# Two graph layers on one core: layer 0's small sums moved from GpSimd to VectorE, and transposes of single pairs one step later

## The chip, the cores and the metric

The kernel runs on one core of a Trainium2 chip. The metric is device time in microseconds (us), lower is better. Engines: PE is TensorE, PEld its weight loads, DVE is VectorE, ACT is ScalarE, POOL is GpSimd, SP is SyncE. "L307" is line 307 of the kernel in question.

## The reference, cut to what matters

```python
# x: 4096 x 512, adj: 4096 x 4096
def layer0(x, adj, weight):
    bw = sign(weight); ba = max(sign(x), 0)
    return relu(adj @ (ba @ bw.T))
x = layernorm(x + layer0(x, adj, w0))

def layer1(x, adj, weight, bias, node_w, edge_w):
    node_att = softmax(x @ node_w, axis=0)
    h = x @ edge_w
    e = where(adj > 0, h @ h.T, NEG_BIG)
    return adj * (node_att * softmax(e, axis=1)) @ (x @ weight) + bias
x = layernorm(x + layer1(...))
```

The whole program has these stretches: layer 0's aggregation `adj @ xw`, then `h`, then the products `h @ h.T` with their softmax statistics, then layer 1's aggregation. The change touches the first and the third.

## The kernel before

Layer 0's aggregation goes by blocks of 128 rows. A block's adjacency arrives in two halves, each half in two chunks. For each chunk, ScalarE makes `hi` (the rounded value), VectorE makes `lo` (the rest), and PE multiplies both. Beside that runs work for layer 1, two pieces per block: `premask` turns pieces of the adjacency into bf16 masks and stores them.

```python
def premask(queue, left):
    if loaded and (len(bufs) == 2 or len(pieces) == left):
        (r, j, c), a = loaded.popleft()
        m = ...                                   # bf16 view of the same buffer
        tc.keep_in_program_order(nc.vector.tensor_scalar(m, a_, 0.0, NEG_BIG, ALU.is_le, ALU.mult))
        nc.gpsimd.dma_start(mask_d[r][:, c : c + 2, j, :], m)      # store, GpSimd's queue
        bufs.append(a)
    if len(pieces) > left:
        r, j, c = pieces.popleft()
        a = bufs.popleft()                        # must wait until the store from `a` has landed
        queue.dma_start(a, adj[...])              # in layer 0: ScalarE's queue
        loaded.append(((r, j, c), a))

def aggregate(b):
    ...
        for q in range(2):
            nc.scalar.copy(hi, aq)
            nc.vector.tensor_sub(lo, aq, hi.bitcast(F32))
            if q == 0:
                premask(nc.scalar, 28)
            for c in range(QC):                   # 8 x 2 matmuls
                nc.tensor.matmul(acc, hi[:, c, :], xw[:, kb, :], ...)
                nc.tensor.matmul(acc, lo[:, c, :], xw[:, kb, :], ...)
    nc.vector.scalar_tensor_tensor(xb, acc, 0.0, xb, ALU.max, ALU.add)
    layernorm([xb])
    nc.vector.tensor_tensor_reduce(scr, xb, nw_b, ..., accum_out=node_s[:, b : b + 1])   # node score
    nc.gpsimd.tensor_add(scr, xb, bias_b)                                               # bias add
    nc.gpsimd.dma_start(x1_d[ts(b, P), :], scr)
    return xb

def left(b, low, high):                           # once for each pair of blocks
    nc.gpsimd.tensor_sub(s3, l11, l21)
    nc.gpsimd.tensor_add(s1, l22, l21)
    nc.gpsimd.tensor_sub(s2, s1, l11)
    nc.gpsimd.tensor_sub(s4, l12, s2)
    nc.gpsimd.dma_start(to[:, 0, :], l11)         # four stores of operands
    ...
```

There are four buffers for the pieces, `pair` (two), `single` and `ends`. The build reorders instructions within an engine unless they are held with `keep_in_program_order`. In the products, a row's copy to SBUF is followed some "steps" later (calls of `between`) by its transposes on PE:

```python
class Single:
    def main(self, between):
        for i in range(BG):
            for k in range(KD):
                nc.tensor.matmul(pe[...], ...)
                if k % 2 and not (self.diag and i > 1):
                    between()                                     # one step
            nc.scalar.copy(src[:, lo * P :], pe[:, lo * P :])
            turns.append((now[0] + 2, lambda ...: self.mirror.turn(s, src, i)))   # transposes
            ...
```

## Time and profile before

| | before |
|---|---|
| time, median of the first 3 runs | 2068.59 us (2063.06 to 2071.97) |
| profiled execution, span | 2059.6 us |
| layer 0's aggregation, first to last matmul after the start-up | 58.9 to 577 us |
| products, first matmul to layer 1's first aggregation matmul | 684.0 to 1163.1 us |
| DVE / ACT / POOL busy | 67% / 33% / 25% |

The lines of the profile that matter are in the prediction, with how to read each. In a line of waits, "A <- B: total, times, longest" means that A's engine stood idle before A until B was done. In a timeline the columns are start, duration, engine, line, operation, output<-inputs, shapes, count, and in brackets the idle time before it and what ended that.

### The profile page before, as it was taken

How to read it: one execution, taken by the hardware profiler on the slowest of the kernel's cores; microseconds unless marked ns; L12 is line 12 of the kernel's file. 1: busy time of each engine (PE TensorE's matmuls, PEld its weight loads, DVE VectorE, ACT ScalarE, POOL GpSimd, SP SyncE). 2: the span in 40 equal slices, each digit the busy share in tenths (PEclk: the TensorE clock that was granted, in tenths of full speed). 3: DMA queues.
4: the chain of work that ended last, by engine and by line, in shares of the span. 5: the costliest groups of instructions: out<-in, count | busy, mean ns of one | idle time of the engine just before them, and what ended most of it. 6: DMA issues, size and time to landing. Idle time of an engine off the chain costs nothing.

```text
span 2059.6 us, 18124 instructions
## 1 busy us (share of the span) xinstructions
PE 1989.2 (97%) x6108; PEld 1104.0 (54%) x6108; DVE 1370.2 (67%) x1896; ACT 673.0 (33%) x1107; POOL 522.6 (25%) x603
## 2 busy tenths in 40 slices
PE   9999899999998999999999899999999999999997
PEld 6777777777853445555545444444444444444443
DVE  7655566665666457576747688688669666967734
ACT  5322232222310357666768431122111311221100
POOL 0443434343543011111112211241215111330101
PEclk9999999999999999999999999999999999999999
DMA  8877777777647558577859887676667766775421
GB/s 302 295 262 251 269 270 275 263 253 253 231 163 261 204 193 287 215 256 281 292 192 366 310 298 261 218 255 240 239 229 246 255 234 213 258 250 209 174 82 61
DMA packets 133644, 497.70 MB, mean 242 GB/s; under 512 B 14000, under 2 KB 14000, under 8 KB 125872
## 3 DMA queue, kind: packets, MB, share of 16 engines
q0 software_dynamic: 71488, 262.17, 34.2%
q1 hardware_dynamic: 54000, 206.07, 29.8%
q10 hardware_dynamic: 8064, 28.32, 4.0%
q8 instruction: 48, 0.79, 0.2%
q14 instruction: 44, 0.36, 0.1%
HBM read 376.96 MB, written 119.54 MB: 241 GB/s over the span
## 4 chain that ended last, share of the span: by engine, by line
PE 70%; DMA 9%; issue 7%; POOL 6%; DVE 4%; ACT 2%; ACTq 0%; POOLq 0%; SPq 0%; DVEq 0%
PE ps L850 37%; PE seven L664 11%; PE po L903 5%; DMA mask_d<-ends 4%; PE seven L98 4%; PE acc L300 3%; PE acc L299 3%; PE pe L595 2%; POOL scr L307 2%; PE pt L565 2%; DMA s_d<-slot 1%; DMA mask_d<-pair 1%; ACT hi L292 1%; DVE lo L294 1%; PE acc L236 1%
## 5 line engine op out<-in xcount | busy, mean ns | idle before, releaser
L850 PE MATMUL ps<-lent,lop 128*128 128x512 f32 x992 | 432.6, 592 | 0.0
L299 PE MATMUL acc<-xw,hi 128*128 128x512 f32 x960 | 390.9, 407 | 26.2 <-ACT hi L292 26.2
L300 PE MATMUL acc<-xw,lo 128*128 128x512 f32 x960 | 389.7, 406 | 11.1 <-DVE lo L294 10.9
L850 PE MATMUL ps<-slot,lop 128*128 128x512 f32 x800 | 351.9, 594 | 0.0
L850 PEld LDWEIGHTS ps<-lent,lop 128*128 128x128 f32 x992 | 188.3, 190 | 236.3 <-issue 231.8
L850 PEld LDWEIGHTS ps<-slot,lop 128*128 128x128 f32 x800 | 152.2, 191 | 190.0 <-issue 185.2
L294 DVE TENSOR_TENSOR lo<-at,hi 128x1024 fp32r<-128x1024 f32 x120 | 155.5, 1297 | 148.1 <-ACT hi L292 148.0
L292 ACT CAST hi<-at 128x1024 fp32r<-128x1024 f32 x120 | 125.9, 1049 | 320.4 <-PE acc L299 202.8
L299 PEld LDWEIGHTS acc<-xw,hi 128*128 128x128 f32 x960 | 188.4, 196 | 69.8 <-ACT hi L292 31.3
L300 PEld LDWEIGHTS acc<-xw,lo 128*128 128x128 f32 x960 | 188.4, 196 | 57.6 <-DVE lo L294 18.2
L854 DVE TENSOR_TENSOR over<-over,ps 128x512 f32<-128x512 f32 x168 | 113.5, 680 | 90.2 <-PE ps L850 90.2
L595 PE MATMUL pe<-hT 128*128 128x512 f32 (+3 forms) x384 | 132.3, 486 | 0.0
L767 ACT ACTIVATE lent<-lent 128x2048 f32<-128x2048 f32 x33 | 62.9, 1910 | 192.5 <-DVE lent L764 189.1
L536 ACT ACTIVATE line<-line,nmax_c 128x512 f32<-128x512 f32 x160 | 114.8, 724 | 33.1 <-DVE nmax_c L527 33.1
L767 ACT ACTIVATE slot<-slot 128x2048 f32<-128x2048 f32 x31 | 59.3, 1911 | 201.1 <-DVE slot L764 201.1
L903 PE MATMUL po<-over 128*128 128x512 f32 x256 | 115.9, 600 | 3.2 <-DVE xb L912 3.2
L527 DVE CUSTOM_DVE_ANT_0 line<-lent,slot 128x512 f32<-128x512 bf16 x144 | 93.0, 688 | 37.0 <-ACT slot L605 19.7
L764 DVE CUSTOM_DVE_ANT_1 slot<-slot,line 128x2048 f32<-128x2048 f32 x31 | 75.2, 2425 | 49.1 <-DMA slot<-s_d 47.6
L764 DVE CUSTOM_DVE_ANT_1 lent<-lent,line 128x2048 f32<-128x2048 f32 x33 | 83.0, 2519 | 23.4 <-DMA lent<-s_d 22.2
L664 PE MATMUL seven<-hT 128*128 128x512 f32 x192 | 89.5, 593 | 0.0
L565 PEld LDWEIGHTS pt<-ident,lent 128*128 128x128 f32 x422 | 52.0, 141 | 63.3 <-issue 39.6
L595 PEld LDWEIGHTS pe<-hT 128*128 128x128 f32 x384 | 64.6, 191 | 37.9 <-issue 31.0
(197 smaller groups left out, 2611.0 us busy)
## 6 DMA issues: line engine op xcount, KB each, us to landing
at<-in_adj_t_dram SPq DMA_DIRECT2D x60, 1024.0 KB, 6.3
lop<-lop_d SPq DMA_DIRECT2D x112, 512.0 KB, 3.6
lent<-in_adj_t_dram POOLq DMA_DIRECT2D x35, 1024.0 KB, 6.9
s_d<-slot POOLq DMA_DIRECT2D x34, 1024.0 KB, 7.6
lent<-s_d POOLq DMA_DIRECT2D x33, 1024.0 KB, 7.3
slot<-s_d POOLq DMA_DIRECT2D x31, 1024.0 KB, 7.8
slot<-in_adj_t_dram POOLq DMA_DIRECT2D x29, 1024.0 KB, 7.5
lent<-in_adj_dram SPq DMA_DIRECT2D x48, 512.0 KB, 5.6
```

The costliest lines, as they stand in the source:

```text
L292: nc.scalar.copy(hi, aq)
L294: nc.vector.tensor_sub(lo, aq, hi.bitcast(F32))
L299: nc.tensor.matmul(acc, hi[:, c, :], xw[:, kb, :], start=(kb == 0), stop=False)
L300: nc.tensor.matmul(acc, lo[:, c, :], xw[:, kb, :], start=False, stop=(kb == NB - 1))
L536: nc.scalar.activation(line, line, AF.Exp, bias=nmax_c[:, b, c : c + 1], scale=-1.0, accum_out=sum_c[:, b, c : c + 1])
L595: nc.tensor.matmul(pe[:, lo * P :], hT[:, k, ts(A * BG + i, P)], hT[:, k, (B * BG + lo) * P : (B + 1) * W], start=(k == 0), stop=(k == KD ...
L664: nc.tensor.matmul(ps, left[m][:, k, q, :], right[m][:, k, :], start=(first and k == 0), stop=(k == KD // 2 - 1), skip_group_check=not first,)
L764: nc.vector._custom_dve(TENSOR_ADD_SAT, out=q, in0=q, in1=mrow.unsqueeze(1).to_broadcast([P, BG, W]), s0=0.0, s1=-HUGE)
L767: nc.scalar.activation(q, q, AF.Exp)
L850: nc.tensor.matmul(ps, lop[:, c, ts(h, P)], rop[:, c, :], start=(c == 0), stop=(c == BG - 1))
L854: nc.vector.tensor_add(total[:, m, h, :], total[:, m, h, :], ps)
L903: nc.tensor.matmul(po, (lower if k // 2 else upper)[:, k % 2, ts(i, P)], w1_s[:, k, :], start=(k == 0), stop=(k == KD - 1),)
```

## The change

Its intent: GpSimd should only begin stores in layer 0, so that none stands behind arithmetic; and in the products, PE should come to a transpose later, when the copy it reads is done, with one step also at the end of each of the last two rows of a diagonal product (the other rows had it).

```diff
@@ aggregate
-            nc.gpsimd.tensor_add(scr, xb, bias_b)
+            nc.vector.tensor_add(scr, xb, bias_b)
@@ left
-            nc.gpsimd.tensor_sub(s3, l11, l21)
-            nc.gpsimd.tensor_add(s1, l22, l21)
-            nc.gpsimd.tensor_sub(s2, s1, l11)
-            nc.gpsimd.tensor_sub(s4, l12, s2)
+            nc.vector.tensor_sub(s3, l11, l21)
+            nc.vector.tensor_add(s1, l22, l21)
+            nc.vector.tensor_sub(s2, s1, l11)
+            nc.vector.tensor_sub(s4, l12, s2)
@@ Single.main
-                    if k % 2 and not (self.diag and i > 1):
+                    if k == KD - 1 or k % 2 and not (self.diag and i > 1):
                         between()
-                turns.append((now[0] + 2, lambda i=i, s=s, src=src: self.mirror.turn(s, src, i)))
+                turns.append((now[0] + 3, lambda i=i, s=s, src=src: self.mirror.turn(s, src, i)))
```

## The prediction

> **What bounds the kernel now.** I read the page's busy times and slices first, then busy time by stretch, then the waits of layer 0's aggregation, then each engine's timeline through one pair of its row blocks.
>
> ```profile
> PE 1989.2 (97%) x6108; PEld 1104.0 (54%) x6108; DVE 1370.2 (67%) x1896; ACT 673.0 (33%) x1107; POOL 522.6 (25%) x603
> PE   9999899999998999999999899999999999999997
> POOL 0443434343543011111112211241215111330101
> ```
>
> TensorE (PE) is busy 97% of 2059.6 us, so only its idle time and its slow-clock time can be won. The slices with an 8 or a lone dip lie mostly in the first quarter, exactly where GpSimd (POOL) is busiest. By stretch (columns: length, then busy us and count of each engine, granted clock, DMA share, GB/s):
>
> ```profile
> 140.00:240.00 100.00, 92.20 (x391) 73.75 (x390) 60.07 (x75) 28.42 (x35) 38.77 (x46) 0.95 0.76 264
> 340.00:440.00 100.00, 89.20 (x363) 71.06 (x362) 59.82 (x73) 25.82 (x32) 42.30 (x47) 0.91 0.75 259
> 517.00:577.00 60.00, 60.00 (x272) 49.37 (x271) 36.97 (x46) 18.54 (x23) 32.53 (x30) 1.00 0.62 224
> ```
>
> The last stretch is the same aggregation after the mask work has ended: no idle PE, clock 1.00. Before it PE idles 8 to 11% and also loses clock. From 59 to 577 us PE issues 1920 aggregation matmuls and 120-odd transposes. The matmuls start 0.227 us apart when nothing stalls (timeline, 240.14 then 240.37), so 1920 x 0.227 = 436 us, and transposes take some 19 us (0.6 for four). 518 - 455 leaves about 63 us lost. Cross-check: PE busy in those 518 us sums to 481, so 37 us idle; the clock averages 0.95, some 25 us more. Sum 62. From 577 us on, PE is nearly gapless, so a gain there is small, and what layer 0 wins simply moves the end forward.
>
> ```profile
> ACT hi L292 <- DMA mask_d<-ends: 74.5, 9, 9.9
> PE acc L299 <- ACT hi L292: 26.2, 12, 4.1
> ACT hi L292 <- DMA mask_d<-pair: 20.0, 5, 4.9
> PE acc L300 <- DVE lo L294: 10.9, 14, 2.2
> ```
>
> The 37 us are two lines: PE waits for ScalarE's (ACT) cast `hi` and then for VectorE's (DVE) `lo`; and `hi` waits for the landing of a mask store. ScalarE also issues the adjacency loads, in order, and a load into `ends` may not start until the mask stored from `ends` has landed; the cast behind it stands still. Why that store is late is in GpSimd's timeline:
>
> ```profile
> 275.40 0.73 POOL L317 TENSOR_TENSOR sums_l<-xb 128x256 f32<-128x256 f32 x1 [3.48 <-DVE xb L154]
> 276.09 0.72 POOL L321 DMA_DIRECT2D lop_d<-xb  x1
> 276.83 2.15 POOL L307 TENSOR_TENSOR scr<-xb,bias_b 128x512 f32<-128x512 f32 x1
> 278.94 1.19 POOL L318 TENSOR_TENSOR sums_l<-sums_l,xb 128x256 f32<-128x256 f32 x1
> 280.07 0.57 POOL L308 DMA_DIRECT2D x_d<-scr  x1
> 280.67 1.25 POOL L319 TENSOR_TENSOR sums_l<-xb,sums_l 128x256 f32<-128x256 f32 x1
> 281.87 0.77 POOL L323 DMA_DIRECT2D lop_d<-sums_l  x1
> 282.63 0.57 POOL L322 DMA_DIRECT2D lop_d<-sums_l  x1
> 283.19 0.71 POOL L272 DMA_DIRECT2D mask_d<-ends  x1
> ```
>
> The normalised row is there at 275.3; the mask of `ends` was ready at 279.5 and its store begins at 283.19, behind 5.3 us of arithmetic. It lands at 290.4, and ScalarE follows:
>
> ```profile
> 290.86 1.04 ACT L292 CAST hi<-at 128x1024 fp32r<-128x1024 f32 x1 [7.24 <-PE acc L300]
> ```
>
> Its buffer had been free since about 286.2 (the cast before started at 282.58, one chunk is 16 x 0.227 = 3.6 us). This recurs once in each pair of row blocks, some 12 times, at 4 to 7 us each.
>
> **What the Trainium skill says.** "GPSIMD Engine Reference", section 3.1, gives GpSimd about 2.6 cycles an element for a two-input add against VectorE's 1, a measured ratio of 1.96. Here the 128x512 add takes 2.18 us (median of 31) on GpSimd; a VectorE add of that shape takes 0.69 (layer 1's groups). The trace is worse than the page. "SBUF — State Buffer", section "Who interferes with whom", has VectorE and GpSimd exclude each other on a shared port pair, for two-port modes and for two-input VectorE operations against GpSimd reads. It agrees:
>
> ```profile
> L271 DVE TENSOR_SCALAR single<-single x13: 685/687/691, 93.0 to 515.2; 128x1024 bf16<-128x1024 f32 x13
> L271 DVE TENSOR_SCALAR ends<-ends x13: 1769/1778/1787, 101.2 to 523.1; 128x1024 bf16<-128x1024 f32 x13
> ```
>
> (Minimum/median/maximum ns.) The same mask operation takes 1.78 us every time it meets the bias add L307, and 0.69 where GpSimd only issues. "TensorE: Matmul & The Clock Gate", Part 1, says that an idle window of some 3.4 us halves the clock. After 4.13 us of idling at 257.84 the matmuls here start 0.43 us apart instead of 0.227. "DMA: Bandwidth & Descriptors", section "Queues, rings and completion order", has the engines go round between queues packet by packet. This trace shows a 256 KB mask store landing in 2.6 us alone (271.19) and in 7.2 to 8.8 us behind the operand stores.
>
> **The change, part by part.** *Removed from GpSimd* per pair: two bias adds of 2.18 and four 128x256 combinations (0.72, 0.73, 1.19, 1.14), 8.1 us. Between the row and the late store lie 5.3 of them (0.73 + 2.15 + 1.19 + 1.25).
>
> *Added to VectorE* per pair: two adds of 0.69 and four combinations. For 128x256 I extrapolate from 0.69 at 512 columns and 1.22 at 1024: 0.42 us each. Sum 1.38 + 1.68 = 3.1 us. *Given back to VectorE:* two of the four masks in a pair fall from 1.78 to 0.69, and some `lo` subtractions from 1.6 or 1.75 to 1.22, so 2.2 to 2.7 us. VectorE's 60% hardly changes.
>
> *The path:* after the row, VectorE would do the node score (1.3 us to its end), the add (0.69), three combinations (1.26, the fourth uses the earlier row alone), `lo` (1.22) and the mask (0.69): 5.2 us. GpSimd's begins fit beside that (0.72 + 0.57 + 0.77 + 0.57 = 2.6). The store of `ends` then begins at +5.2 instead of +7.9, 2.7 us earlier. The operand and row stores in front of it also start earlier, by 2.5 to 3.5 us, while the load before (landed 280.42) is ending and before the next big one (281.35) begins, so less is queued ahead. I estimate 3 to 5 us on the landing. The need: 3 to 3.5 us where a stall now costs 4 to 5 us in all, and 5.3 us in the worst (256.7: PE dry at 253.5, `lo` at 259.1). I choose 4: seven small stalls vanish, five big ones keep about 2 us each, 10 us.
>
> *New waits:* the `lo` after the row comes some 1.9 us later: row + 4.4 us, and PE wants it at +3.9. That is up to 0.5 us in each of 15 pairs, 6 us with the odd one beside it, too short for the clock to fall. Layer 0: 62 - 10 - 6 = 46 us; because the instruction order may change with the engines, I count 38.
>
> *Second part:* in the last products (1138 to 1163 us) PE waits for ScalarE's copies before transposes: 2.65, 0.84, 1.90, 2.25 us, with one slow-clock stretch of 1.7, and 1.16 at 1012. One step later puts two matmuls (about 0.9 us) in front of a transpose, so at most 4 to 5 us; but ScalarE is held by exponentials that wait for VectorE, and additional steps in diagonal products hand VectorE more early work. I take 3 us.
>
> Sum: 38 + 3 = 41 us, so 2068.6 - 41 = about 2028 us.
>
> **Rivals.** *(a) DMA takes the wait over.* Each pair moves about 9.3 MB, 270 GB/s over some 34.5 us now; at 31 us it is 300. For it: mask stores already land three times slower in company. Against: the slices reach 366 GB/s. If landings stretch by 2 us, the gain is 20 us: 2048. *(b) VectorE becomes the wait.* The combinations stand ahead of `lo`, with two buffers and 1.4 us of slack in each 3.6 us chunk. For: `lo` already waits behind the node score. Against: masks get faster by as much. If each row block lost 1 us: 30 us, gain 14, 2054. *(c) Everything vanishes:* all 12 stalls with their clock loss, the `lo` slipped in ahead of the combinations, 60 us and 5 from the second part: 2004. *(d) The second part backfires:* later transposes make later mirror statistics, and the last products end 5 us later: 2033 with the rest as estimated.
>
> **Range and chances.** (a) and (b) set the top at 2052, most of (c) the bottom at 2008. The 2% line is 2027.2, at my estimate, so faster and same are near even; slower would need a cost of 41 us that no part has, 0.02.
>
> **What would show it.** Right: no GpSimd arithmetic in layer 0's rows, every L271 near 0.69 us, ScalarE's wait for mask stores falling from 94 us to under 30, PE's wait for `hi` from 26 to under 8, clock of the aggregation stretch from 0.95 to 0.98 or more, hidden layer start some 38 us earlier, and small new waits for `lo`. Wrong: mask stores beginning 2.7 us earlier but landing no earlier (a), or PE's wait for `lo` over 20 us (b). The prediction fails as a whole if the stores stay behind waits for VectorE in GpSimd's queue as long as they stood behind its arithmetic.

## The result, and the profile after

The changed kernel took 2013.65 us (median of 4 runs, 2009.32 to 2018.92) against 2065.82 (median of 4, 2060.96 to 2071.97). The ratio is 0.9747 with a 95% interval of 0.9709 to 0.9785: faster by 2.5%. A ratio here is the mean time of one kernel's runs over that of the other's of the same rounds, so it is not quite the ratio of the medians. All outputs are right. The profiled execution of the changed kernel is its slowest (2018.92, span 2017.2), and that of the kernel before is near the fast end of its runs (2061.74), so the traces show 42 us of the difference.

The page of the changed kernel: busy times, then PE's and GpSimd's busy tenths in 40 slices.

```profile
PE 1969.7 (98%) x6108; PEld 1094.7 (54%) x6108; DVE 1353.9 (67%) x1992; ACT 673.0 (33%) x1107; POOL 398.2 (20%) x507
PE   8999999999999999999999899999999999999997
POOL 0212121221341011111122211240134111421101
```

GpSimd's load in the first quarter is halved, PE's dips there are gone from the slices. VectorE has 96 more instructions and yet is busy 16 us less (1370.2 before). By stretch (length, busy us and count of PE, PEld, DVE, ACT, POOL, then clock, DMA share, GB/s):

```profile
140.00:240.00 100.00, 97.10 (x424) 79.15 (x423) 62.59 (x100) 31.22 (x38) 19.77 (x30) 0.97 0.83 291
340.00:440.00 100.00, 96.89 (x428) 79.09 (x429) 63.50 (x101) 30.04 (x37) 21.04 (x32) 0.98 0.82 290
```

PE is busy 97% instead of 92 and 89%, and does 424 and 428 matmuls in 100 us instead of 391 and 363. From its first to its last matmul the aggregation takes 59.9 to 533.7 us, 474 us, 44 less. The other stretches keep their lengths: `h` 106.2 us (106.6 before), the products 479.9 (479.1), layer 1's aggregation to the end 896.7 (896.5).

The waits in the changed kernel's aggregation:

```profile
ACT hi L292 <- DMA mask_d<-pair: 34.6, 8, 5.0
ACT hi L292 <- DMA at<-in_adj_t_dram: 22.1, 3, 8.0
ACT rstd L151 <- DMA mask_d<-pair: 14.8, 4, 4.2
PE acc L300 <- DVE lo L294: 7.3, 11, 1.1
PE acc L299 <- ACT hi L292: 6.2, 4, 2.3
```

PE's waits have gone from 37.1 us to 13.5. ScalarE still waits 34.6 + 14.8 us for mask stores. The three waits of the second line, which end at 201.3, 298.3 and 394.3 us, are put down to an adjacency load. But in each the load into `ends` began only 0.5 us before (at 297.85 in the second), when the store from `ends` had landed (297.79), and the adjacency load landed later (298.46). So all three are the old wait. GpSimd after a pair's second row:

```profile
255.91 0.71 POOL L321 DMA_DIRECT2D lop_d<-xb  x1 [3.63 <-DVE xb L154]
257.58 0.58 POOL L308 DMA_DIRECT2D x_d<-scr  x1 [0.96 <-DVE scr L307]
258.16 0.74 POOL L323 DMA_DIRECT2D lop_d<-sums_l  x1
259.39 0.58 POOL L322 DMA_DIRECT2D lop_d<-sums_l  x1 [0.48 <-DVE sums_l L319]
260.00 0.71 POOL L272 DMA_DIRECT2D mask_d<-ends  x1
```

The row is ready at 255.6 and the store of `ends` begins 4.4 us later; before it was 7.9. It lands at 265.29, 9.7 us after the row instead of 15.1. Over all pairs of the two traces the medians are 4.4 us instead of 7.8 for the begin and 10.6 instead of 15.3 for the landing. ScalarE now meets it in time:

```profile
265.36 0.33 ACTq L277 DMA_DIRECT2D ends<-in_adj_dram  x1
266.32 1.05 ACT L292 CAST hi<-at 128x1024 fp32r<-128x1024 f32 x1 [2.57 <-PE acc L299]
```

The cast's wait ends with PE's release of its buffer, not with a landing. And VectorE's operations when nothing collides any more (minimum/median/maximum ns), the mask, and the node score after and before:

```profile
L271 DVE TENSOR_SCALAR ends<-ends x13: 684/686/691, 98.7 to 481.4; 128x1024 bf16<-128x1024 f32 x13
L304 DVE CUSTOM_DVE_ANT_0 scr<-xb,nw_b x32: 691/693/694, 62.2 to 538.9; 128x512 f32<-128x512 f32 x32
```
```profile
L304 DVE CUSTOM_DVE_ANT_0 scr<-xb,nw_b x32: 692/1248/1256, 61.2 to 581.9; 128x512 f32<-128x512 f32 x32
```

### The profile page after: what moved, and what is told of

Its sections match the earlier page's. It is cut to its first block, busy times and chain, and to the rows that moved or that the text cites. A ratio compares the mean times of both kernels' runs of the same rounds, so it can differ in the third digit from the quotient of the medians.

```text
span 2017.2 us, 18164 instructions
## 1 busy us (share of the span) xinstructions
PE 1969.7 (98%) x6108; PEld 1094.7 (54%) x6108; DVE 1353.9 (67%) x1992; ACT 673.0 (33%) x1107; POOL 398.2 (20%) x507
## 4 chain that ended last, share of the span: by engine, by line
PE 69%; issue 17%; DMA 5%; DVE 4%; POOL 4%; ACT 2%; POOLq 0%; ACTq 0%; DVEq 0%; SPq 0%
PE ps L850 38%; PE seven L664 12%; PE po L903 5%; PE seven L98 4%; PE acc L300 2%; PE pe L595 2%; PE acc L299 2%; DMA s_d<-slot 2%; PE pt L565 2%; POOL mask_d L272 1%; PE acc L236 1%; ACT line L536 1%; PE acc L237 1%; PE pw L206 1%; POOL x_d L308 1%
## 5 line engine op out<-in xcount | busy, mean ns | idle before, releaser
L850 PE MATMUL ps<-lent,lop 128*128 128x512 f32 x976 | 425.7, 592 | 0.0
L300 PE MATMUL acc<-xw,lo 128*128 128x512 f32 x960 | 379.7, 396 | 7.3 <-DVE lo L294 7.3
L299 PE MATMUL acc<-xw,hi 128*128 128x512 f32 x960 | 379.8, 396 | 6.2 <-ACT hi L292 6.2
L850 PE MATMUL ps<-slot,lop 128*128 128x512 f32 x816 | 359.0, 594 | 0.0
L294 DVE TENSOR_TENSOR lo<-at,hi 128x1024 fp32r<-128x1024 f32 x120 | 146.5, 1221 | 120.0 <-ACT hi L292 119.8
L300 PEld LDWEIGHTS acc<-xw,lo 128*128 128x128 f32 x960 | 182.5, 190 | 49.4 <-DVE lo L294 11.8
L299 PEld LDWEIGHTS acc<-xw,hi 128*128 128x128 f32 x960 | 182.5, 190 | 44.2 <-ACT hi L292 7.2
L151 ACT ACTIVATE rstd<-mv,eps 128x1 f32<-128x1 f32 (+1 forms) x43 | 12.6, 295 | 242.1 <-DVE mv L149 210.5
L903 PEld LDWEIGHTS po<-over 128*128 128x128 f32 x256 | 49.1, 192 | 65.9 <-issue 59.9
```

Source lines behind the costliest of these rows:

```text
L299: nc.tensor.matmul(acc, hi[:, c, :], xw[:, kb, :], start=(kb == 0), stop=False)
L300: nc.tensor.matmul(acc, lo[:, c, :], xw[:, kb, :], start=False, stop=(kb == NB - 1))
L850: nc.tensor.matmul(ps, lop[:, c, ts(h, P)], rop[:, c, :], start=(c == 0), stop=(c == BG - 1))
L903: nc.tensor.matmul(po, (lower if k // 2 else upper)[:, k % 2, ts(i, P)], w1_s[:, k, :], start=(k == 0), stop=(k == KD - 1),)
```

## The experiments

Two questions were open. Which part of the change earned the time? And what is the cost that layer 0 got rid of: ScalarE standing still for a late landing (theory W), or VectorE being slowed by GpSimd's arithmetic (rival C)? Twelve kernels ran, in three sets; the kernels of a set shared the runs of the kernel before (medians 2061.42, 2061.78 and 2062.41 us).

### e1_layer0_only: the layer 0 part alone

The first two hunks of the diff, without the third.

> Only the layer 0 part of the change (bias add and four combinations on VectorE). Theory L (all of the gain is in layer 0: the aggregation stretch went from 518 to 474 us between the two traces, while the products from 684 to 1163 us took 479 us before and 480 after): ratio to before within 0.003 of the full change's 0.975, some 2013 us, aggregation about 474 us, last products still about 479 us. Rival S (the later transposes and additional steps earn part of it): this kernel stays 5 us or more above the full change, 2019 or later.

Measured: 2013.83 us (2009.26 to 2016.06, 5 runs), ratio 0.9768 (0.9744 to 0.9792). In its trace the aggregation takes 473 us and the products 479. This is the changed kernel's time. Theory L holds.

### e2_steps_only: the second part alone

The third hunk alone, on the kernel before.

> Only the second part (transposes one step later, additional steps in diagonal products), layer 0 as before. Theory L: ratio to before 0.998 to 1.002, the products take 479 us give or take 3. My recorded prediction gave this part 3 us (ratio 0.9985). Rival S: 5 us or more faster, ratio under 0.9975.

Measured: 2061.49 us (2049.94 to 2066.56, 6 runs), ratio 0.9996 (0.9969 to 1.0022); products 479.0 us. The second part moves nothing that can be seen here; the interval leaves room for 6 us faster or 5 us slower. Layer 0 itself varies from run to run: the profiled run is the fastest of its six, and its aggregation is 505 us long where the kernel before, with the same layer 0, showed 518.

### e3_before_fifth_buffer: one buffer more for the pieces, first attempt

```diff
-        bufs = deque([pair[:, 0, :], pair[:, 1, :], single, ends])
+        fifth = wp.tile([P, 2 * W], F32, name="fifth")
+        bufs = deque([pair[:, 0, :], pair[:, 1, :], single, ends, fifth])
+        spare = [3]
...
-            if loaded and (len(bufs) == 2 or len(pieces) == left):
+            if loaded and (len(bufs) == spare[0] or len(pieces) == left):
```

(To make room, the warm-up tile shares the buffer of `scr`; `spare` goes back to 2 when the buffers are handed over to `h`.)

> The kernel before with a fifth buffer for the mask pieces, so that the load into a buffer waits for a store made one half row block (some 7.3 us) earlier. GpSimd's arithmetic stays in its place, and so do its collisions with VectorE: ends-type masks still 1.78 us where they meet the bias add. Theory W (what cost time is only that ScalarE waits for the landing of a late store): the aggregation falls from 518 us to under 485, ScalarE's wait for mask stores from 94 us to under 15, ratio 0.975 to 0.985. Rival C (the slowing of VectorE by GpSimd's arithmetic is what mattered, the landing wait only a symptom): the aggregation stays above 500 us, because VectorE delays lo as before, ratio above 0.99.

Measured: 2059.03 us (4 runs), ratio 0.9988 (0.9965 to 1.0012), the aggregation as long as before. By its expectation this spoke for rival C. But the trace shows that the premise had not been met. GpSimd's store from `fifth`, and ScalarE's next load into it:

```profile
248.36 0.71 POOL L274 DMA_DIRECT2D mask_d<-fifth  x1
...
256.11 0.33 ACTq L279 DMA_DIRECT2D fifth<-in_adj_dram  x1
256.55 1.04 ACT L294 CAST hi<-at 128x1024 fp32r<-128x1024 f32 x1 [8.82 <-DMA mask_d<-fifth]
```

The load waits for the store that was begun just before it (landing 256.05), although in the program three other pieces come in between. All nine loads into `fifth` that follow such a store begin within 0.1 us of its landing. So the build seems to have answered the additional buffer by moving each load further ahead, again right behind its own store. The test is void: the wait it was to remove is still there.

### e4_after_fifth_buffer: the same on the changed kernel

> The changed kernel with the fifth buffer. The changed kernel's trace still has three stalls at 203, 300 and 396 us that together cost about 15 us, two of them behind a mask store's landing. Theory W: these vanish, aggregation 460 to 464 us, ratio to before 0.967 to 0.971 (about 2003 us). Rival D (they come from the busier DMA, whatever the buffers): aggregation stays at 470 or more, ratio as the changed kernel's, 0.973 to 0.977.

Measured: 2018.92 us (2010.08 to 2029.19, 6 runs), ratio 0.9795 (0.9766 to 0.9823); void for the same reason (here, too, all nine loads into `fifth` begin within 0.1 us of a store's landing). It is no better than the changed kernel.

### e5_before_pinned_loads: the load held in its place

The kernel before with this and nothing else:

```diff
-                queue.dma_start(a, adj[ts(r * BG + j, P), c * W : (c + 2) * W])
+                load = queue.dma_start(a, adj[ts(r * BG + j, P), c * W : (c + 2) * W])
+                if left:
+                    tc.keep_in_program_order(load)
```

> The kernel before, with one thing held: in layer 0 ScalarE's load of the next mask piece keeps its place in the program. In the fifth-buffer run the build had moved each load right behind the store from its own buffer, so no distance was gained and the test was void; here the load of a piece follows the store from its buffer by two half row blocks, some 14 us. GpSimd's arithmetic and its collisions stay. Theory W (ScalarE standing still for a late landing is the cost): ScalarE's wait for mask stores falls from 94 us to under 10, the aggregation from 505 to 518 us to under 480, ratio 0.975 to 0.985. Rival C (VectorE slowed by GpSimd's arithmetic is the cost): the aggregation stays above 500, ratio above 0.99.

Measured: 1996.24 us (1993.87 to 2001.01, 4 runs), ratio 0.9687 (0.9663 to 0.9711). One held load gains 3.1%, more than the whole change, with all of GpSimd's arithmetic in its old place. By stretch, the mask operation, and a store of `ends`:

```profile
140.00:240.00 100.00, 100.00 (x454) 82.80 (x453) 69.64 (x87) 33.39 (x40) 47.12 (x53) 1.00 0.89 316
340.00:440.00 100.00, 100.00 (x456) 82.77 (x455) 69.28 (x86) 33.54 (x41) 48.77 (x55) 1.00 0.87 310
```
```profile
L271 DVE TENSOR_SCALAR ends<-ends x14: 684/1777/1779, 98.7 to 528.9; 128x1024 bf16<-128x1024 f32 x14
```
```profile
283.44 0.71 POOL L272 DMA_DIRECT2D mask_d<-ends  x1
```
```profile
293.52 0.34 ACTq L277 DMA_DIRECT2D ends<-in_adj_dram  x1
294.88 1.05 ACT L294 CAST hi<-at 128x1024 fp32r<-128x1024 f32 x1 [2.58 <-PE acc L301]
```

PE is busy 100% at clock 1.00. The masks still collide (median 1.78 us). The store of `ends` still begins late, 7.4 us after its row (276.08; 7.9 in the pair shown of before), and lands even later, at 293.50, 10 us after its start. ScalarE's load into `ends` starts right then; but now the next cast is not wanted before 294.88, so nobody waits. Loads into `single`, which used to begin within 0.1 us of the landing too, now begin 7.0 to 8.9 us after it. The two waits for mask stores have vanished from the list of waits of the stretch. Theory W holds in its strong form, and rival C falls: collisions of VectorE and GpSimd much as before (node score 1.25 us, as before) cost nothing here. The gain is above the expected 1.5 to 2.5% because all of the some 62 us went, not most of them.

### e6_layer0_part_pinned_loads: both remedies

The layer 0 part of the change, with the load held.

> The layer 0 part of the change with ScalarE's loads held in place as in the run before. Theory W: the rest of the waits for mask stores goes too, some 19 us of loss in the aggregation fall to 8 to 12, aggregation 462 to 466 us, ratio 0.970 to 0.974, so 5 us or so below the layer 0 part alone. If the two remedies take away the same wait and nothing else, they do not add up: ratio within 0.003 of 0.977.

Measured: 1994.57 us (1993.17 to 1995.36, 4 runs), ratio 0.9676 (0.9660 to 0.9691). This is 19 us below the layer 0 part alone (2013.83), more than either expectation allowed, and within 2 us of the held load alone. The two remedies take away the same wait; the held load takes all of it, the change some 70%.

### e7_bias_only: the bias adds alone

> Only the bias adds on VectorE, the four combinations stay on GpSimd. Theory W, by lateness: of the 5.3 us of arithmetic between the row and the store of ends this takes away 2.15; a gain of 15 to 25 us, ratio 0.987 to 0.993. Rival C, by collisions: it is the bias add that the masks meet, so nearly all of the gain comes from it, 35 us or more, ratio under 0.983.

Measured: 2040.23 us (2033.29 to 2042.21, 4 runs), ratio 0.9892 (0.9869 to 0.9915): 22 us. Inside W's band, outside C's.

### e8_combinations_only: the four combinations alone

> Only the four combinations on VectorE, the bias adds stay on GpSimd. Theory W, by lateness: 3.2 of the 5.3 us go, a gain of 20 to 30 us, ratio 0.985 to 0.990. Rival C: the masks still meet the bias add and take 1.78 us, the gain stays under 8 us, ratio above 0.996.

Measured: 2034.05 us (2030.51 to 2036.75, 4 runs), ratio 0.9867 (0.9848 to 0.9886): 28 us. Inside W's band. C's premise failed here, though: in the new order the masks hardly meet the bias add any more (`ends` 0.68 us at the maximum), so this run alone doesn't speak against C. The two halves add up, 22 + 28 = 50 us against 48 for the layer 0 part: each microsecond of GpSimd arithmetic that went from in front of the store (2.15 and 3.2) was worth 9 to 10. That is a proportion and not a mechanism shown, for in e8 PE's waits for `lo` rose from 10.9 to 20.6 us while those for `hi` fell from 26.2 to 7.7.

### e9 to e12: the second part on a quiet base

With layer 0 quiet, the runs of one kernel lie 2 to 8 us apart, so the second part can be taken to pieces. The base first:

> The layer 0 part with held loads once more, as the base for the three runs beside it: its four times lay within 2.2 us (1993.2 to 1995.4), so 2 us can be seen on it. Expected: ratio 0.966 to 0.969, products 479 us.

Measured: 1996.07 us (1993.21 to 2000.92, 4 runs), ratio 0.9683; products 478.9 us in its trace. This is the kernel of e6 once more, which gave 1994.57 us and 478.6: two sets of the same kernel differ by 1.5 us.

The transposes later, without the additional steps (`now[0] + 3` alone):

> That base with the transposes one step later, and no more steps in diagonal products. Theory M (PE's waits before transposes are only moved to another transpose, since ScalarE's copies are late by exponentials that wait for VectorE): within 1.5 us of the base. Theory O (the delay earns the 3 us of my prediction and the additional steps take them back): 2.5 to 4 us below the base.

Measured: 1993.78 us (1990.85 to 1996.60, 5 runs), ratio 0.9670 (0.9651 to 0.9689); products 475.9 us.

The additional steps, without the delay (the condition on `k` alone):

> That base with the additional steps in diagonal products, transposes as before. Theory M: within 1.5 us of the base. Theory O: 2.5 to 4 us above it.

Measured: 1998.86 us (1997.56 to 2000.11, 4 runs), ratio 0.9694 (0.9676 to 0.9711); products 480.9 us.

Both, that is the whole change with held loads:

> The whole change with held loads. Theories M and O both: within 1.5 us of the base, so 1993 to 1997 us, ratio 0.966 to 0.969. If both parts help once layer 0 is quiet: 3 us or more below.

Measured: 1995.54 us (1994.06 to 1998.28, 4 runs), ratio 0.9679 (0.9661 to 0.9697); products 479.6 us.

Medians and the lengths in the traces tell the same: the delay takes 2.3 us off the time and 3.0 off the products, the steps put 2.8 and 2.0 on, both together change it by -0.5 and +0.7. This points to theory O, two parts that cancel, though the delay's 2.3 us lies between theory M's band (under 1.5) and theory O's (2.5 to 4). The runs of delay alone (up to 1996.60) and of steps alone (from 1997.56) do not overlap. But each of them overlaps the base, the intervals of the ratios overlap, and each length is from one trace, so it is not settled. PE's longest waits in the products (first the base, then delay alone, then steps alone):

```profile
PE pt L567 <- ACT lent L607: 7.7, 4, 2.7
```
```profile
PE pt L567 <- ACT lent L607: 4.2, 1, 4.2
```
```profile
PE ptm L736 <- ACT slot L568: 3.0, 1, 3.0
PE pt L567 <- ACT lent L607: 2.4, 2, 2.0
```

With the delay, four waits of 7.7 us become one of 4.2, with another of 2.2 us for a different copy. With the steps, those waits shrink too, but PE waits 3.0 us for the transposes of `spread`, which layer 1's early work asks for. All of PE's waits from 940 to 1110 us sum to 9.1 us in the base, 7.7 with the delay and 7.9 with the steps, so the waits alone do not explain why the steps lengthen the products. In that trace the granted clock was half for 3.4 us from 1050.3 and again from 1064.0 us, each time just behind a wait. With the delay there is one such stretch (1086.7), and in the base's products none. By estimate the two cost half of 6.8 us. That the steps cost time because they bring early work forward is argued, not shown by a run of its own.

## Why the prediction was right or wrong

**The bound and the mechanism: right.** Some 62 us were said to be lost in layer 0's aggregation, behind ScalarE's wait for a late mask store. The held load (e5) removed this wait and left GpSimd's arithmetic where it was; it gained 66 us, and its trace shows PE at 100% from 140 to 500 us. So the 62 us were there, and were this wait's.

**Layer 0's sum: right, but the discount was mis-sized.** The working gave 62 - 10 - 6 = 46 us, then "I count 38" for changes of order. The aggregation became 44 us shorter in the traces, and the layer 0 part alone made it 48 us faster. Of the 63 us lost, 19 are left (474 - 455), where 10 + 6 were expected: 13.5 of PE's waits and, by estimate, 6.8 from 13.7 us at half clock. The order did change, but harmlessly: the build put `lo` of the following chunk ahead of the fourth combination. The time, 2013.65, is 14 us below the predicted 2028. Of these, 2.8 are the kernel before, whose median was 2065.82 in this comparison and 2068.59 when I predicted. The gain was 52 us by medians instead of 41: 8 more by the discount, 3 less by the second part, and 6 that lie in the spread of runs, for the same difference is 42 us between the two traces and 48 in e1's set.

**Its steps.** The store begins 3.5 and 3.0 us earlier in the two pairs I compared (4.4 and 4.9 us after the row, against 7.9), where 2.7 was worked out; it lands 5.4 and 3.2 us earlier, where 3 to 5 was estimated (4.7 by the medians over all pairs). The VectorE durations came out as extrapolated, 0.42 and 0.68 us. What I missed is that the node score also shrank, from 1.25 to 0.69 us in nearly every block: it is an operation with two inputs that had met GpSimd's combinations. (In e7, where the combinations stay on GpSimd, it takes 0.69 us as well; there the first combinations are the ones that stretch, from 0.72 to 1.23 us.) Together with the masks that is why VectorE's total fell. The new waits for `lo`, 6 us in the prediction, came to about 2: three of them, at 65.6, 132.2 and 452.4 us, stand behind moved operations and sum to 2.1 us. In all, PE's waits for `lo` fell from 10.9 to 7.3 us.

The prediction ties the slow clock to an idle window of some 3.4 us, with a wait of 4.13 us as its case. The traces show it after shorter waits too: after 1.20 and 0.76 us at 150.4 and 151.7 us in the kernel before, and after 1.02 and 0.76 us at 395.4 and 396.6 in the changed one, the granted clock was 0.50 for 3.4 us. After 1.62 and 0.77 us at 203.4 in e1 it stayed at 1.00. So here the measurement differs from the page that the prediction cites, and the length of one wait does not decide; what does was not tried.

**A check that failed.** ScalarE's waits for mask stores were to fall from 94 us to under 30. They fell to 49, and with the three of the second waits line it is about 70. (The 94 was too small in the same way: three of the twelve waits for stores of `ends`, 20.9 us with the one of 7.24 that the prediction shows, are put down to PE there.) PE's waits fell all the same, because a wait of ScalarE that ends within PE's stock of one prepared chunk costs nothing. The sum of an engine's waits was the wrong thing to watch.

**The second part: the sum was wrong.** From "at most 4 to 5 us" for the delay, 1 to 2 were taken off for ScalarE's exponentials and for the additional steps, which left 3. The delay alone measures 2.3 to 3.0 us. The step that failed is the size of what was taken off: the additional steps, named as a risk, seem to take 2 to 3 us back by themselves. The part as a whole shows no gain (0.9996).

**The rivals.** (a), DMA as the new bound: not so, e5 moves 316 GB/s with PE at 100%. Its landings do stretch, to 10 us, and it does not matter there. (b), VectorE as the wait: not so, PE's waits for `lo` are 7.3 us and not over 20; only e8, with the combinations alone, reached its sign (20.6). (c), everything vanishes: not with this change, but the 60 us it named are about what e5 and e6 gained (66 and 67 us). (d), the second part backfires by 5 us: neither seen nor quite excluded by e2's interval; e12 against e9 shows no loss.

**Sums and readings that do not come out.** In (d), 5 us lost in place of 3 gained makes 2036, not 2033. In (b), 41 - 30 leaves a gain of 11, not 14, and its 2054 lies above the top of 2052 that it was to set. The twelve late stores of `ends` landed in 5.7 to 9.1 us, not 7.2 to 8.8. None of them moves the 2028.

**What stays open.** The changed kernel keeps four stalls of PE behind `hi`, at 108, 202, 299 and 395 us, one in each third pair of blocks (before there were twelve); why there was not tried. Nor is it known why the fifth buffer made the changed kernel's runs spread to 2029 us.

## What to carry to other kernels

When an engine that feeds the critical path also issues loads, look for the place of each load in that engine's queue: one that waits there for a landing holds up everything behind it, however fast the stores are made. Try to move the wait before speeding up what it waits for; here holding one load in program order gained 3.1%, and moving all of the arithmetic away 2.5% or less. An additional buffer is worth nothing if the build answers by moving the load forward by as much, so read the order that came out, not the one that was written.

## What the Trainium skill lacked or had wrong

- "DMA: Bandwidth & Descriptors", section "Issuing engines are not separate DMA queues", says that initiating DMAs on several engines only saves the sequencer's time, which is usually small. That page doesn't say that a load waiting for its buffer stands in the issuing engine's queue ahead of computation (the life of a DMA instruction in "Perfetto Trace Analysis" has the sequencer hold that wait, without this consequence): ScalarE stood 7.2 us before one cast for this, and holding the load in another place of the same queue took 66 us off 2062 (e5).
- "GPSIMD Engine Reference", section 3.1: the ratio 1.96 holds where nothing collides (in e8 the 128x512 bias add has a median of 1.35 us, against 0.68 on VectorE). With VectorE's `lo` and masks beside it the same add took 2.18 us, a ratio of 3.2. The page says elsewhere that the two engines contend, but gives no size for it. In the prediction I took this for a difference between page and chip; e8 speaks for the collision.
- "SBUF — State Buffer", section "Who interferes with whom", agrees with the trace (masks 1.78 against 0.69 us, node score 1.25 against 0.69). It gives no example of collisions that cost nothing: e5 keeps them and has PE at 100%.
- No page has that an additional buffer can be undone by the order of the build ("Trainium Kernel Development and Optimization", section "Best Practices", only advises to double-buffer): the fifth buffer gave a ratio of 0.9988.
